# Graph attention scores: 32-row products with keys block-diagonal over two heads, and masks stored by tile

## The chip, the cores and the metric

The kernel runs on one core of a Trainium2 chip (trn2). The metric is the time on the device in microseconds of one execution; the median over several runs counts. TensorE (PE) multiplies matrices into PSUM and loads its weights separately (PEld in the profile). VectorE (DVE), ScalarE (ACT) and GpSimd (POOL) do elementwise work, and SyncE (SP) issues most of the DMAs. All data are fp32.

## What is computed

Two layers follow one another on x, 64 batches of 64 tokens with 256 features: a graph attention in two directions, then a transformer block with modulation. The change concerns the graph attention. Cut to that:

```python
def _gat_attention(self_feat, cond_adj, label_bias, Wq, bq, Wk, bk, Wout, bout):
    B, N, F = self_feat.shape          # 64, 64, 256
    ng = min(NONGT, N)                 # 20 keys per batch
    dh = F // H                        # 16 heads of 16
    kv = self_feat[:, :ng]
    qh = (self_feat @ Wq.T + bq).reshape(B, N, H, dh)
    kh = (kv @ Wk.T + bk).reshape(B, ng, H, dh)
    aff = jnp.einsum('bnhd,bmhd->bnhm', qh, kh) * (1.0 / np.sqrt(dh))
    mask = cond_adj[:, :, None, :] > 0
    aff = jnp.where(mask, aff, NEG) + label_bias[:, :, None, :]
    w = jax.nn.softmax(aff, axis=-1)
    out_t = jnp.einsum('bnhm,bmf->bnhf', w, kv)
    ...
for d in range(2):
    A = adj_f if d == 0 else jnp.swapaxes(adj_f, 1, 2)
    A = A[:, :, :NONGT, :]             # 11 labels per pair
    cond = A.sum(-1)
    vb = A @ w_bias + b_bias
    output = output + _gat_attention(self_feat, cond, vb, ...)
```

The second layer is layer norm with a modulation, 16-head attention over the 64 tokens of a batch, and an MLP with a hidden width of 1024, each with a gated residual.

## The kernel before

**Tiling.** Tokens are worked on in groups: one of 4 batches, seven of 8 and one of 4. A group is cut into tiles of 128 tokens, two batches each (`s` counts them), 32 tiles in all. Feature-major tensors have 256 features in two chunks `c` of 128 partitions. The schedule is written out by hand: the order of the calls is the order of each engine's instructions.

**The pipeline.** `period(g)` runs the transformer attention of group g beside the graph attention of group g+1, the MLP of group g-1 and preparation of group g+2. Its unit is `slot`: block scores of one tile (`block_scores`, line 620), graph scores of one tile (`graph_scores`, line 458), and then, interleaved, the softmax of both on DVE, ACT and POOL, the transposes and weighted sums of the tiles of the slot before, and pieces of the MLP as filling (`fills`). `boundary` stands between groups. `start` works on the graph tiles of the first group, and on the first two of the second group, ahead of the first slots; there are 28 slots with both kinds of scores, and `finish` has no graph scores.

**Graph scores.** For each direction `d` and chunk `c`, `graph_q` (lines 422 and 423) makes the queries qT, and `graph_k` (lines 407 and 411) the keys kT, feature-major; 128 partitions hold eight heads of 16. Heads are separated by a block-diagonal form of the keys. `graph_keys` multiplies kT with a mask that keeps one of four heads in each of four copies, so that 64 partitions (four heads) against 4 x 20 = 80 columns give the scores of four heads in one product. It is one POOL instruction a tile (line 441), except in the second group, where it is four ACT instructions (line 436). `graph_scores` then makes 16 products a tile: 2 directions, 2 chunks, 2 row groups `r` of 64 partitions, 2 batches `s`. The queries are the weights (64 rows, 64 columns), the key blocks the moving operand (80 columns).

**PSUM.** Two pairs of banks, sca and scb, take the scores. Block scores use columns 0 to 255 of all four banks: the row groups 0 and 1 of 32 partitions have the two banks of sca, 2 and 3 those of scb. Graph scores lie behind them in the same banks; direction 0 is in sca and direction 1 in scb, and each row group has its own bank of the pair.

**Softmax of the graph tile.** `mask_step` sums the labels of the adjacency on DVE (line 347, count) and the weighted labels (line 352), and makes from them `keep` (line 356) and `term` (lines 359 and 360), stored by direction, then tile, then key. `graph_masked` multiplies PSUM by keep, one DVE instruction a direction (line 469), and adds term on POOL (line 474). `graph_exp` takes maxima and subtracts on DVE (lines 479, 480), and exponentiates on ACT (line 481). `graph_normal` sums, inverts and scales (lines 486 to 488). `graph_turned` transposes on PE (line 496); `graph_output` multiplies with the values (line 514), adds on DVE (line 523), ACT (line 524) and POOL (line 525).

**Other lines of the prediction.** Block scores' maxima and subtraction on DVE are lines 631 and 633, their scaling on POOL line 645 (pr), the transposes line 656 (ppT), the weighted sum line 667 (pao). Line 605 makes the block-diagonal keys of the transformer attention on POOL, 32 partitions and two heads a product. Line 242 is the projection of the conditioning. Lines 737 and 747 are the two products of the MLP.

The order of the heads in the columns of Wq and Wk is arranged on the host, in `kernel`, so that the products leave the heads in natural order.

Of the kernel before, what the change touches and what calls it, by code (L numbers as in the profile page):

```python
# [9 lines left out]
F32 = mybir.dt.float32  # L10
I32 = mybir.dt.int32
AF = mybir.ActivationFunctionType
ALU = mybir.AluOpType
AX = mybir.AxisListType
# [3 lines left out]
P = 128  # L18
B, N, D = 64, 64, 256
H, HD = 16, 16  # L20
M = 20
L = 11
# [24 lines left out]
def graph_attention_then_dit_block(  # L47
# [22 lines left out]
    nc = tc.nc  # L70
# [5 lines left out]
    two = ctx.enter_context(tc.tile_pool(name="two", bufs=2))  # L76
# [118 lines left out]
    hmask4 = const.tile([P, 4], F32, name="hmask4")  # L195
    nc.gpsimd.tensor_tensor(hmask4, hmask[:, 0:4], hmask[:, 4:8], ALU.add)

    hmask2 = const.tile([P, 2], F32, name="hmask2")
# [139 lines left out]
    def mask_step(g, i):  # L338
        G = groups[g]
        rows = G.nt * M  # L340
        d, what = divmod(i, 3)
        if i == 0:
            G.cnt = small.tile([P, 2 * NT * M], F32, tag="cnt", name="cnt", bufs=1)[:, 0 : 2 * rows]
            G.vb = small.tile([P, 2 * NT * M], F32, tag="vb", name="vb", bufs=1)[:, 0 : 2 * rows]
        a3 = G.adj[d].rearrange("p j (m l) -> p (j m) l", l=L) if d < 2 else None
        if d < 2 and what == 0:
            nc.vector.tensor_reduce(G.cnt[:, ts(d, rows)], a3, AX.X, ALU.add)
        elif d < 2 and what == 1:

            nc.vector.tensor_tensor(a3.bitcast(F32), a3, wb.unsqueeze(1).to_broadcast([P, rows, L]), ALU.mult)  # L350
        elif d < 2:
            nc.vector.tensor_reduce(G.vb[:, ts(d, rows)], a3.bitcast(F32), AX.X, ALU.add)
        else:
            keep_f = small.tile([P, 2 * NT * M], F32, tag="keep", name="keep")[:, 0 : 2 * rows]
            G.keep = keep_f.rearrange("p (d j m) -> p d j m", d=2, m=M)
            nc.vector.tensor_scalar(keep_f, G.cnt, 0.0, None, ALU.is_gt)
            term_f = small.tile([P, 2 * NT * M], F32, tag="term", name="term")[:, 0 : 2 * rows]
            G.term = term_f.rearrange("p (d j m) -> p d j m", d=2, m=M)
            nc.vector.tensor_scalar(term_f, keep_f, -1.0, -NEG, ALU.add, ALU.mult)
            nc.vector.scalar_tensor_tensor(term_f, G.vb, bb, term_f, ALU.add, ALU.add)  # L360

# [67 lines left out]
    def graph_keys(g, j):  # L429

        G = groups[g]
        G.kblk = getattr(G, "kblk", {})
        kblk = G.kblk[j] = two.tile([P, 2, 2, 2, 4 * M], F32, tag="kblk", name="kblk")
        if g == 1:
            for h in range(4):
                nc.scalar.activation(
                    kblk.rearrange("p d c s (h m) -> p h (d c s) m", h=4)[:, h],
                    G.kT[:, j].rearrange("p d c (s m) -> p (d c s) m", s=2), AF.Copy, scale=hmask4[:, h : h + 1],
                )
            return  # L440
        nc.gpsimd.tensor_tensor(
            kblk.rearrange("p d c s (h m) -> p (d c s) h m", h=4),
            G.kT[:, j].rearrange("p d c (s m) -> p (d c s) m", s=2).unsqueeze(2).to_broadcast([P, 8, 4, M]),
            hmask4.unsqueeze(1).unsqueeze(3).to_broadcast([P, 8, 4, M]), ALU.mult,
        )

    def graph_scores(g, j, sc, first=4 * N):

        G = groups[g]
        t = Tile()  # L450
        t.g, t.j = g, j
        t.pa = [p_[:, :, ds(first, 8 * M)] for p_ in sc]
        kblk = G.kblk[j]
        for d in range(2):
            for c in range(2):
                for r in range(2):
                    for s in range(2):
                        nc.tensor.matmul(  # L458
                            t.pa[d][ts(s, N), r, ts(c, 4 * M)],
                            G.qT[ts(r, 64), d, c, ds(j * P + s * N, N)],  # L460
                            kblk[ts(r, 64), d, c, s, :], start=True, stop=True,
                        )
        return t

    def graph_masked(t):
        G, j = groups[t.g], t.j
        t.w = two.tile([P, H, 2, M], F32, tag="w", name="w")
        for d in range(2):
            nc.vector.tensor_tensor(  # L469
                t.w[:, :, d, :].rearrange("p (r h) m -> p r h m", r=2),  # L470
                t.pa[d].rearrange("p r (h m) -> p r h m", h=8),
                G.keep[:, d, j, :].unsqueeze(1).unsqueeze(1).to_broadcast([P, 2, 8, M]), ALU.mult,
            )
        nc.gpsimd.tensor_tensor(t.w, t.w, G.term[:, :, j, :].unsqueeze(1).to_broadcast([P, H, 2, M]), ALU.add)  # L474

    def graph_exp(t):
        wf = t.w.rearrange("p h d m -> p (h d) m")
# [287 lines left out]
    def slot(e, c, e_next, c_next, before, fill, late=False):  # L765
        Eb, Cb = before
        fill("p")
        sc = [pair("pa", "sca"), pair("pb", "scb")] if e or c else None
        E = block_scores(*e, sc) if e else None
        C = graph_scores(*c, sc) if c else None  # L770
        fill("p2")
        if Eb:
# [6 lines left out]
        if c_next and c_next[0] != 1:  # L779
            graph_keys(*c_next)  # L780
        if E:
            block_exp(E)
        if c_next and c_next[0] == 1:
            graph_keys(*c_next)
        if C:
            graph_masked(C)
# [31 lines left out]
    def boundary(g, before):  # L818
# [8 lines left out]
        if c_on:  # L827
            graph_v(g + 1, 1)
            if g == 1:
                half_normed(1, 3)  # L830
            for i in {1: (3, 1, 2, 4), 2: (1, 2, 4)}.get(g, (4, 5, 6)):
                mask_step(g + 1, i)
# [14 lines left out]
        if g <= 2:  # L847
            mask_step(g + 1, 5)
            mask_step(g + 1, 6)
# [48 lines left out]
        if c_on:  # L898
            graph_keys(g + 1, 0)
# [137 lines left out]
    def start():  # L1037
# [19 lines left out]
        for d in range(2):  # L1057
            for c in range(2):
                graph_q(0, d, c)
        sc = [pair("pa", "sca"), pair("pb", "scb")]  # L1060
        t0 = [graph_scores(0, 0, sc), graph_scores(0, 1, sc, 0)]
        for t in t0:
            graph_masked(t)
# [45 lines left out]
        graph_q(1, 1, 1)  # L1109
        sc = [pair("pa", "sca"), pair("pb", "scb")]  # L1110
        t1 = [graph_scores(1, 0, sc), graph_scores(1, 1, sc, 0)]
        for t in t1:
            graph_masked(t)
# [208 lines left out]
```

## Time and profile before

| | us |
|---|---|
| median of 3 runs | 672.87 |
| lowest, highest | 672.36, 674.28 |
| span of the profiled execution | 672.5 |

The span goes from the first to the last instruction of one profiled execution; durations are taken from it. The groups that the change touches, with their number of instructions and the mean time of one:

| line, engine | what | count | ns of one |
|---|---|---|---|
| 458 PE | graph scores, matmuls of 64x64, 80 columns | 1024 | 230 to 241 |
| 458 PEld | their weight loads | 1024 | 133 |
| 620 PE | block scores, 32x64, 128 columns | 1024 | 281 |
| 441 POOL | key blocks, 640 elements | 28 | 1252 |
| 436 ACT | key blocks of the second group, 160 elements | 16 | 416 |
| 469 DVE | scores times keep, 320 elements | 64 | 482 |
| 474 POOL | plus term, 640 elements | 32 | 1547 |
| 347 DVE | counts, up to 880 elements in | 18 | up to 1060 |
| 352 DVE | label bias, up to 880 elements in | 18 | up to 1071 |

How to read the views: a matmul's duration contains its way through the array, so durations of neighbouring matmuls overlap and can't be summed; their starts show the rate. An fp32 product appears as two pairs of load and matmul. A row of the timeline merges instructions of a line that follow closely: its start, its length, the engine, line and operation, output and inputs, shapes, and x how many; brackets give the idle time of the engine before it and what ended it. A row of the table by stretches gives, behind the length, the busy time and number of instructions of PE, PEld, DVE, ACT and POOL, then the granted clock of PE, the share of DMA and GB/s.

### The profile page before, as it was taken

The numbers are of one execution on the slowest core, as the hardware profiler recorded it, in microseconds if no ns is written. First come the engines' busy times: TensorE is split into PE (matmuls) and PEld (weight loads), VectorE is DVE, ScalarE is ACT, GpSimd is POOL, SyncE is SP. The second block draws the span as 40 slices with busy tenths as digits, with TensorE's granted clock in tenths as the row PEclk, the third lists the DMA queues.
The fourth block names the chain that finished last, engine by engine and source line by source line (L and its number), as shares of the span: only waits on it lengthen the run. The fifth ranks groups of instructions, "written<-read, shape, count | busy, mean of one in ns | idle before, by whom it ended". The sixth has DMA issues, their size and how long they took to land.

```text
span 672.5 us, 15456 instructions
## 1 busy us (share of the span) xinstructions
PE 657.7 (98%) x6422; PEld 405.7 (60%) x6422; DVE 473.3 (70%) x863; ACT 354.5 (53%) x627; POOL 369.9 (55%) x366
## 2 busy tenths in 40 slices
PE   8999898999999999999999999999999999999997
PEld 7657656775555555556556555555565575566446
DVE  4988866997777677775876867876778766666221
ACT  3355437663665437644476436664376544864412
POOL 5555447666674466654584556754766555545210
PEclk9999899999999999999999999999999999999999
DMA  7636031004000220004000041002100000000000
GB/s 244 201 90 203 22 104 18 18 22 135 17 2 34 90 68 17 18 17 156 1 18 17 22 153 17 1 18 73 42 9 12 19 25 2 2 2 17 17 16 32
DMA packets 34655, 33.42 MB, mean 50 GB/s; under 512 B 5625, under 2 KB 28409, under 8 KB 34585
## 3 DMA queue, kind: packets, MB, share of 16 engines
q1 hardware_dynamic: 34104, 32.33, 15.5%
q8 instruction: 51, 0.84, 0.6%
q14 instruction: 20, 0.16, 0.1%
q10 hardware_dynamic: 416, 0.09, 0.1%
q0 software_dynamic: 64, 0.01, 0.0%
HBM read 25.59 MB, written 6.83 MB: 48 GB/s over the span
## 4 chain that ended last, share of the span: by engine, by line
PE 86%; DVE 7%; ACT 3%; POOL 2%; issue 1%; DMA 1%; SPq 0%; DVEq 0%; ACTq 0%; POOLq 0%
PE py L747 15%; PE pu L737 15%; PE pqT L422 8%; PE pqk L582 8%; PE ppT L656 4%; PE pv L590 4%; PE pwT L496 3%; PE pf L324 3%; PE pproj L692 3%; PE po L514 3%; PE pk L407 2%; PE pao L667 2%; PE pv L371 2%; PE sca L620 2%; PE phT L560 2%; PE pxT L533 2%
## 5 line engine op out<-in xcount | busy, mean ns | idle before, releaser
L747 PE MATMUL py<-u,w 128*128 128x512 f32 (+1 forms) x272 | 118.3, 562 | 0.2 <-ACT u L739 0.2
L737 PE MATMUL pu<-h2T,w 128*128 128x512 f32 (+1 forms) x256 | 108.9, 570 | 0.4 <-ACT v L597 0.4
L645 POOL TENSOR_TENSOR pr<-pr,sm 128x1024 f32<-128x1024 f32 x32 | 60.9, 1902 | 73.0 <-DVE sm L644 53.5
L474 POOL TENSOR_TENSOR w<-w,term 128x640 f32<-128x640 f32 x32 | 49.4, 1547 | 71.1 <-DVE w L469 39.5
L737 PEld LDWEIGHTS pu<-h2T,w 128*128 128x128 f32 x256 | 47.6, 190 | 48.2 <-issue 42.6
L747 PEld LDWEIGHTS py<-u,w 128*128 128x128 f32 x272 | 47.7, 190 | 36.9 <-issue 33.2
L422 PE MATMUL pqT<-sfT,wq 128*128 128x512 f32 (+1 forms) x144 | 61.7, 558 | 0.3 <-DVE y L715 0.3
L739 ACT ACTIVATE u<-pu,vec 128x512 f32<-128x512 f32 (+1 forms) x72 | 43.1, 640 | 33.5 <-PE pu L737 33.3
L582 PE MATMUL pqk<-hT,wqkv 128*128 128x512 f32 (+1 forms) x144 | 59.5, 550 | 0.5 <-POOL hT L569 0.4
L631 DVE TENSOR_REDUCE mx<-sca 128x8 f32<-128x512 f32 x32 | 22.0, 688 | 48.8 <-PE sca L458 47.4
L481 ACT ACTIVATE w<-w 128x640 f32<-128x640 f32 x32 | 23.6, 736 | 56.9 <-DVE w L480 55.9
L641 DVE TENSOR_REDUCE sm<-pr 128x16 f32<-128x1024 f32 x32 | 38.9, 1216 | 20.3 <-ACT pr L637 20.0
L423 ACT ACTIVATE qT<-pqT,vec 128x512 f32<-128x512 f32 (+1 forms) x36 | 23.0, 639 | 51.8 <-PE pqT L422 51.7
L659 ACT COPY pT<-ppT 128x512 f32<-128x512 f32 x64 | 34.5, 591 | 26.4 <-PE ppT L656 26.4
L637 ACT ACTIVATE pr<-pr 128x1024 f32<-128x1024 f32 x32 | 33.8, 1057 | 27.2 <-DVE pr L633 27.0
L546 POOL TENSOR_TENSOR rstd<-rstd,mhalf 128x2 f32<-128x2 f32 x32 | 23.3, 727 | 41.7 <-DVE rstd L545 40.8
L583 ACT ACTIVATE qk<-pqk,vec 128x512 f32<-128x512 f32 (+1 forms) x36 | 23.0, 639 | 43.0 <-PE pqk L582 43.0
L488 POOL TENSOR_TENSOR w<-w,sm 128x640 f32<-128x640 f32 x32 | 44.1, 1380 | 1.9 <-DVE sm L487 1.8
L551 DVE TENSOR_SCALAR xn<-xn,mv,rstd 128x256 f32<-128x256 f32 x64 | 37.9, 632 | 10.0 <-POOL rstd L546 10.0
L542 DVE BATCH_NORM_STATS2 st<-xn 128x6 f32<-128x256 f32 x64 | 26.1, 408 | 24.3 <-ACT xn L535 24.2
L525 POOL TENSOR_TENSOR xT<-xT,sfT 128x256 f32<-128x256 f32 x32 | 23.2, 726 | 34.1 <-ACT sfT L524 29.0
L500 ACT COPY wT<-pwT 80x512 f32<-80x512 f32 x64 | 33.9, 581 | 13.0 <-PE pwT L496 12.9
(148 smaller groups left out, 1432.5 us busy)
## 6 DMA issues: line engine op xcount, KB each, us to landing
xT<-in_x_t SPq DMA_DIRECT2D x7, 512.0 KB
out<-xT SPq DMA_DIRECT2D x14, 256.0 KB
a_d<-in_adj SPq DMA_DIRECT2D x7, 440.0 KB
a_d<-in_adj_t SPq DMA_DIRECT2D x7, 440.0 KB
x_g<-in_x SPq DMA_DIRECT2D x5, 512.0 KB
vblk<-vd SPq DMA_DIRECT2D x28, 80.0 KB
w<-in_w SPq DMA_DIRECT2D x2, 1024.0 KB
vd<-v_sb SPq DMA_DIRECT2D x7, 256.0 KB
```

Source lines behind the costliest of these rows:

```text
L422: nc.tensor.matmul(pq, wq_sb[d][:, k, ts(c, P)], G.sfT[:, k, :], start=(k == 0), stop=(k == 1))
L474: nc.gpsimd.tensor_tensor(t.w, t.w, G.term[:, :, j, :].unsqueeze(1).to_broadcast([P, H, 2, M]), ALU.add)
L488: nc.gpsimd.tensor_tensor(wf, wf, sm.unsqueeze(2).to_broadcast([P, 2 * H, M]), ALU.mult)
L500: nc.scalar.copy(t.wT[:, ts(q4, 4), :], pt[0 : 4 * M, :].rearrange("p (i t) -> p i t", i=4))
L551: nc.vector.tensor_scalar(key.xn[:, i, :], key.xn[:, i, :], key.mv[:, i, 0:1], key.rstd[:, i : i + 1], ALU.subtract, ALU.mult,)
L582: nc.tensor.matmul(pp, wqkv_sb[:, k, ds(i * D + c * P, P)], G.hT[:, k, 0 : G.T], start=(k == 0), stop=(k == 1))
L641: nc.vector.tensor_reduce(t.sm, t.pr, AX.X, ALU.add)
L645: nc.gpsimd.tensor_tensor(t.pr, t.pr, t.sm.unsqueeze(2).to_broadcast([P, H, N]), ALU.mult)
L659: nc.scalar.copy(t.pT[:, ts(q4, 4), :], pt.rearrange("p (i t) -> p i t", i=4))
L737: nc.tensor.matmul(pu, w1_sb[:, k, ts(m, P)], G.h2T[:, k, 0 : G.T], start=(k == 0), stop=(k == 1))
L739: nc.scalar.activation(G.u[m], pu, AF.Gelu, bias=col("b1", m))
L747: nc.tensor.matmul(G.py, w2_sb[:, m, ts(c, P)], G.u[m], start=(m == 0), stop=(m == 7))
```

## The change

Graph scores become 32 products of 32 rows a tile. The key blocks hold two heads in place of four: 40 columns instead of 80, and half the size. The row groups `q` of 32 partitions take the four banks of sca and scb (q 0 and 1 in sca, 2 and 3 in scb), and both directions of a row group lie in its bank, with the direction inside the head: chunk, head, direction, key. An output is therefore two runs of 20 columns, 40 apart. The weights are 32 rows of queries and 64 columns. The position in the array is given: row 32q, column 64s, the same as for the block scores.

`keep` and `term` are stored by tile, then direction, then key, so that the 40 values of a tile lie together; the reductions that make the count and the label bias write runs of 20 accordingly. The masked product is cut by row groups instead of directions: each of the two DVE instructions still has 320 elements, and writes a contiguous half of `w`. The sum on POOL takes the 40 values as one run. Key blocks are made with the mask for two heads: one POOL instruction of 320 elements, or two ACT instructions in place of four. On the host the heads of Wq and Wk take the order that the transformer attention has already.

```diff
@@ mask_step
+        a4 = G.adj[d].rearrange("p j (m l) -> p j m l", l=L) if d < 2 else None
+
+        def by_direction(flat):
+            return flat.rearrange("p (j d m) -> p j d m", d=2, m=M)[:, :, d]
+
         if d < 2 and what == 0:
-            nc.vector.tensor_reduce(G.cnt[:, ts(d, rows)], a3, AX.X, ALU.add)
+            nc.vector.tensor_reduce(by_direction(G.cnt), a4, AX.X, ALU.add)
...
-            nc.vector.tensor_reduce(G.vb[:, ts(d, rows)], a3.bitcast(F32), AX.X, ALU.add)
+            nc.vector.tensor_reduce(by_direction(G.vb), a4.bitcast(F32), AX.X, ALU.add)
...
-            G.keep = keep_f.rearrange("p (d j m) -> p d j m", d=2, m=M)
+            G.keep = keep_f.rearrange("p (j r) -> p j r", j=G.nt)
...
-            G.term = term_f.rearrange("p (d j m) -> p d j m", d=2, m=M)
+            G.term = term_f.rearrange("p (j r) -> p j r", j=G.nt)
@@ graph_keys
-        kblk = G.kblk[j] = two.tile([P, 2, 2, 2, 4 * M], F32, tag="kblk", name="kblk")
+        kblk = G.kblk[j] = two.tile([P, 2, 2, 2, 2 * M], F32, tag="kblk", name="kblk")
         if g == 1:
-            for h in range(4):
+            for h in range(2):
                 nc.scalar.activation(
-                    kblk.rearrange("p d c s (h m) -> p h (d c s) m", h=4)[:, h],
-                    G.kT[:, j].rearrange("p d c (s m) -> p (d c s) m", s=2), AF.Copy, scale=hmask4[:, h : h + 1],
+                    kblk.rearrange("p d c s (h m) -> p h (d c s) m", h=2)[:, h],
+                    G.kT[:, j].rearrange("p d c (s m) -> p (d c s) m", s=2), AF.Copy, scale=hmask2[:, h : h + 1],
                 )
             return
         nc.gpsimd.tensor_tensor(
-            kblk.rearrange("p d c s (h m) -> p (d c s) h m", h=4),
-            G.kT[:, j].rearrange("p d c (s m) -> p (d c s) m", s=2).unsqueeze(2).to_broadcast([P, 8, 4, M]),
-            hmask4.unsqueeze(1).unsqueeze(3).to_broadcast([P, 8, 4, M]), ALU.mult,
+            kblk.rearrange("p d c s (h m) -> p (d c s) h m", h=2),
+            G.kT[:, j].rearrange("p d c (s m) -> p (d c s) m", s=2).unsqueeze(2).to_broadcast([P, 8, 2, M]),
+            hmask2.unsqueeze(1).unsqueeze(3).to_broadcast([P, 8, 2, M]), ALU.mult,
         )
@@ graph_scores
         for d in range(2):
             for c in range(2):
-                for r in range(2):
+                for q in range(4):
+                    out4 = t.pa[q // 2][:, q % 2].rearrange("p (c h d m) -> p c h d m", c=2, h=2, d=2)
                     for s in range(2):
                         nc.tensor.matmul(
-                            t.pa[d][ts(s, N), r, ts(c, 4 * M)],
-                            G.qT[ts(r, 64), d, c, ds(j * P + s * N, N)],
-                            kblk[ts(r, 64), d, c, s, :], start=True, stop=True,
+                            out4[ts(s, N), c, :, d], G.qT[ts(q, 32), d, c, ds(j * P + s * N, N)],
+                            kblk[ts(q, 32), d, c, s, :].rearrange("p (h m) -> p h m", h=2),
+                            start=True, stop=True, tile_position=(32 * q, 64 * s),
                         )
@@ graph_masked
-        for d in range(2):
+        wf = t.w.rearrange("p h d m -> p h (d m)")
+        for i in range(2):
             nc.vector.tensor_tensor(
-                t.w[:, :, d, :].rearrange("p (r h) m -> p r h m", r=2),
-                t.pa[d].rearrange("p r (h m) -> p r h m", h=8),
-                G.keep[:, d, j, :].unsqueeze(1).unsqueeze(1).to_broadcast([P, 2, 8, M]), ALU.mult,
+                wf[:, ts(i, 8)].rearrange("p (q h) m -> p q h m", q=2),
+                t.pa[i].rearrange("p q (h m) -> p q h m", h=4),
+                G.keep[:, j].unsqueeze(1).unsqueeze(1).to_broadcast([P, 2, 4, 2 * M]), ALU.mult,
             )
-        nc.gpsimd.tensor_tensor(t.w, t.w, G.term[:, :, j, :].unsqueeze(1).to_broadcast([P, H, 2, M]), ALU.add)
+        nc.gpsimd.tensor_tensor(wf, wf, G.term[:, j].unsqueeze(1).to_broadcast([P, H, 2 * M]), ALU.add)
@@ kernel
-    order = np.arange(D).reshape(2, 2, 4, HD).transpose(1, 0, 2, 3).reshape(-1)
-
     order1 = np.arange(D).reshape(4, 2, 2, HD).transpose(1, 0, 2, 3).reshape(-1)
...
     for name in ("Wq", "bq", "Wk", "bk"):
-        l0[name] = l0[name][:, order]
+        l0[name] = l0[name][:, order1]
```

## The prediction

> **What bounds the kernel now.** I read the busy table and the slices of the page first, then the busy times of four stretches, then the timeline of one slot.
>
> ```profile
> PE 657.7 (98%) x6422; PEld 405.7 (60%) x6422; DVE 473.3 (70%) x863; ACT 354.5 (53%) x627; POOL 369.9 (55%) x366
> ...
> PEclk9999899999999999999999999999999999999999
> ```
>
> ```profile
> 0.00:120.00 120.00, 110.87 (x1168) 78.47 (x1169) 91.82 (x166) 57.06 (x115) 67.50 (x77) 0.99 0.40 124
> 120.00:505.00 385.00, 384.90 (x3859) 227.48 (x3857) 288.15 (x516) 216.27 (x370) 229.56 (x219) 1.00 0.14 42
> ```
>
> PE is the bound: between 120 and 505 us it is busy 384.90 of 385.00 us at the full granted clock, while DVE, ACT and POOL are at 75%, 56% and 60%. There, PE time saved is kernel time saved. In the first 120 us PE is idle for 9 us, so savings can be lost there. The change touches PE at line 458, in 28 slots where the graph scores directly follow the block scores, and twice in the start for two tiles at a time. One of the slots in the timeline (start and length in us; PEld rows are weight loads):
>
> ```profile
> 208.41 0.15 PEld L620 LDWEIGHTS sca<-kb,qk 32*64 32x64 f32 x4 [0.76 <-POOL w L488]
> ...
> 208.49 0.15 PEld L620 LDWEIGHTS scb<-kb,qk 32*64 32x64 f32 x4
> ...
> 208.68 0.29 PE L620 MATMUL sca<-kb,qk 32*64 32x128 f32 x4
> ...
> 208.79 0.29 PE L620 MATMUL sca<-kb,qk 32*64 32x128 f32 x4
> 208.81 0.29 PE L620 MATMUL scb<-kb,qk 32*64 32x128 f32 x4
> 209.03 0.35 PEld L458 LDWEIGHTS sca<-kblk,qT 64*64 64x64 f32 x16 [0.17 <-issue]
> 209.03 0.51 PE L458 MATMUL sca<-kblk,qT 64*64 64x80 f32 x16
> ...
> 209.36 0.46 PE L458 MATMUL scb<-kblk,qT 64*64 64x80 f32 x16
> 209.61 0.69 DVE L631 TENSOR_REDUCE mx<-sca 128x8 f32<-128x512 f32 x1 [3.15 <-PE sca L458]
> 209.74 0.86 PEld L656 LDWEIGHTS ppT<-ident,pr 128*128 128x128 f32 x8
> ```
>
> Each fp32 product shows as two load+matmul pairs, so 16 products are 32 pairs. The block scores (32-row products) run in rounds of eight: rounds start 0.11 us apart (208.68, 208.79), and inside a round four matmuls lie within 0.29 - 0.268 = 0.02 us (one takes 268 ns), so a start every 7 ns. The graph scores (64-row) run in rounds of four: the scb group is 0.46 long, one matmul 0.229, so four rounds span 0.23, or 0.069 a round. Columns explain both: 109/128 and 69/80 ns are 0.85 ns a column. The last block matmul starts at 208.83 and streams until 208.94, yet the first graph load starts at 209.03: 0.09 us of nothing. The last graph matmul starts at 209.59 (209.36 + 0.46 - 0.229), streams 0.07, and again 0.09 passes until 209.74. From the last block matmul to the next load: 0.91 us, the same within 1 ns in 27 of the 28 slots (the other waits for POOL behind it).
>
> **The change on PE.** 32 products of 32 rows and 40 columns replace 16 of 64 rows and 80: 64 pairs, in eight rounds of eight, on the array tiles and the four banks that the block scores use. What limits a round:
> - streaming: 40 x 0.85 = 34 ns;
> - starting eight pairs: 8 x 6.7 = 54 ns, from the 7 ns above;
> - the weights: each array tile needs a new load of 64 columns per round. In the block scores the loads of the second round start 0.055 after those of the first (208.41; 208.46). For loads longer than their matmul in steady state, the nearest row is the time projection, 128-column weights under 64-column matmuls:
>
> ```profile
> 50.13 0.97 PEld L242 LDWEIGHTS pt<-siluT,wt_sb 128*128 128x128 f32 x8
> ```
>
> (0.97 - 0.19)/7 = 0.111 us a load; half the columns make 55 ns, and a few ns more if part of it is fixed for each load. I take 58, the upper end, since this row is the steady one. So a round costs 58 ns where it cost 69, and there are still eight.
>
> The larger part is the seam. Both score stages now have one array layout (32x64). Inside the block scores no seam of 0.09 stands between rounds, nor between the attended product and the graph output (lines 667 to 514, both 32 columns wide): there loads at 228.46 start while the earlier matmuls run. So I take the 0.09 before the graph scores as gone, and their first loads as hidden under the last block round. The new slot: first graph matmul at 208.79 + 0.109 = 208.90; last at 208.90 + 7 x 0.058 + 7 x 0.0067 = 209.35; plus 0.034 streaming and 0.09 of seam, next load at 209.47 instead of 209.74. **0.27 us saved a slot** (0.29 with rounds of 55 ns).
>
> In the start, both pairs of graph tiles wait in mid-stage for the last qT activation (line 423), before and after; behind that wait lie ten rounds: 10 x 0.011 + 0.034 = 0.15 us each. The first pair's gain ends in the 1.0 us wait before the transposes at 25.98, so I count one.
>
> Where is the slot's gain lost? Where the next PE wait hangs on a chain that starts in the same slot. At 112.94 the transposes wait 2.03 us for POOL's pr, whose chain begins with the block scores: nothing gained from slot 110. The slots at 49.4 (PE waits 0.89 at 54.80 for a masked product) and 572.5 (0.48 idle before 578.0) I count out likewise. Elsewhere the slack is large: pr of the slot before 208 ended at 203.62 + 1.90 = 205.5, needed at 209.74.
>
> Sum: 25 x 0.27 + 0.15 = **6.9 us**; at most 28 x 0.29 + 0.3 = 8.4. The profiled span is 672.5 us, 0.4 under the median of the runs; 672.87 - 6.9 = **666.0 us**.
>
> **A rule against it.** TensorE: Matmul & The Clock Gate, section "Back-to-back issue gap", gives 1 to 64 columns a floor of about 60 cycles, some 25 ns start to start, and TensorEngine Tiling (Array Packing), section "Performance Considerations", warns against taking the tiling factor from a dimension that is already small: exactly what 80 to 40 columns does. By that floor as an estimate, 64 pairs would take 1.6 us a slot against 0.56 now, some 29 us in all. The trace has matmuls of different array tiles 7 ns apart, so it doesn't hold across tiles here.
>
> **The parts beside PE**, all off the path while PE is the bound:
> - Key blocks (line 441): POOL's 28 instructions of 1.25 us go from 640 to 320 columns. The 256-column product of line 605 takes 0.61; so 0.61 to 1.25, and I take 0.7: 15 us less on POOL, ahead of the block keys that the scores wait for. On ACT (line 436) eight fewer instructions of 0.42 us. Worth 0 to 0.5 us of PE waits; I take 0.
> - Masked product (line 469): same 320 elements, output now contiguous; 0.42 (line 523, 256 contiguous elements) to 0.48. POOL's sum (line 474): 1.27 (line 488, contiguous) to 1.55. Zero; if DVE became the bound, the most is 64 x 0.06 = 4 us.
> - Count and bias reductions (lines 347, 352): 36 instructions of up to 1.06 us now write in runs of 20. Line 469 already writes such runs, at 1.5 ns an element, no dearer than line 523's 1.6; so 0, at worst 36 x 0.1 = 4 us of DVE time, under DVE's 25% of idleness.
> - Waits: mx (line 631) waits for the last matmul into sca, which used to be the middle of the stage (209.31) and now lies four starts before its end (209.32): unchanged. Behind it on DVE stand the subtractions and masked products. PE's next use of the result is the 4 us slack above. An interleaved store into PSUM (two runs of 20) has no row: 0, or twice the streaming, 68 ns a round, which makes the slot's gain 0.16 and the sum 4.2.
>
> **Rivals.**
> 1. *The seam stays* (the first graph load waits until the array is empty, whatever the layout). Then 209.03 + 0.055 + 7 x 0.058 + 0.047 + 0.124 = 209.66: 0.08 a slot, 2.2 us, **670.7**. For it: every change of line with another layout shows it. Against: 667 to 514.
> 2. *The gain is taken by waits*: PE arrives 0.27 earlier and waits for DVE or POOL. Under 2 us kept, **671 to 673**. Against: nearly no PE idleness from 120 to 505, slack of microseconds.
> 3. *Slower: the pairs can't be fed.* No row shows more than about 64 pairs in a run, and the densest long one (line 667: 32 pairs from 228.04 to 228.46) gives 13.4 ns a pair, though there streaming explains it. At 13.6 ns a pair a round is 0.109, the slot ends 0.134 later: 28 x 0.134 + 2 x 10 x 0.04 = 4.6, **677.5**. It decides from 11.5 ns a pair: the 0.91 us less 0.06 before the first and 0.12 behind the last leave 0.72 for 63 steps. Against: after PE had stood 0.46 us for ACT's qk, eight pairs of line 620 start from 48.98 to 49.06: 10 ns a pair from a standstill.
>
> **Chances.** Forecast 0.70 (664.4 to 668.7, the interleaved store included), seam 0.10, waits 0.08, feed 0.12. The range, 663.8 to 671.0, takes in the first two. A measurement of this kernel tells about 0.3%, 2 us, from no change. Faster: 0.70 + 0.07 of the seam + 0.01 = 0.78; same: 0.03 + 0.07 = 0.10; slower 0.12.
>
> **What would show it.** Line 458 with 2048 matmuls of 32x40; its first load in a slot no longer behind a gap of 0.09 after line 620; rounds 55 to 58 ns apart; last block matmul to next load 0.64 us instead of 0.91; line 441 near 0.7. The forecast is wrong if a round takes over 92 ns, if the gap before line 458 stays, or if new PE idleness between 120 and 505 us exceeds 2 us.

## The result and the profile after

The changed kernel takes **684.75 us** (median of 4 runs, 683.91 to 685.44) where the kernel before takes 673.57 beside it: ratio 1.0164, interval 1.0145 to 1.0184. It is slower by 1.6%, outside the range and on the other side of the forecast. Two experiments further down, e2 and e13, have a profile only of a disturbed execution in which matmuls took two to two and a half times as long; their times and ratios come from their other runs.

From the page of the changed kernel, the busy table and the chain that ended last:

```profile
span 683.5 us, 17497 instructions
...
PE 662.4 (97%) x7446; PEld 413.9 (61%) x7446; DVE 471.0 (69%) x863; ACT 352.2 (52%) x619; POOL 354.6 (52%) x366
...
PE 82%; DVE 7%; ACT 4%; another core or an unknown queue 2%; POOL 2%; issue 1%; DMA 1%; SPq 0%; DVEq 0%; ACTq 0%; POOLq 0%
```

The same two stretches as before (length, then busy time and number of instructions of PE, PEld, DVE, ACT, POOL, granted clock, DMA share, GB/s), and what PE waited for in the second one:

```profile
0.00:120.00 120.00, 111.43 (x1422) 80.50 (x1422) 90.17 (x165) 55.01 (x107) 64.68 (x77) 0.99 0.40 124
120.00:505.00 385.00, 378.18 (x4320) 225.79 (x4311) 280.63 (x505) 207.06 (x358) 210.69 (x212) 1.00 0.14 42
```

```profile
PE pv L597 <- issue: 4.9, 3, 2.7
PE pu L744 <- ACT v L604: 1.1, 1, 1.1
PE ppT L663 <- ACT u L746: 0.6, 2, 0.3
```

PE is idle for 6.82 us between 120 and 505 us where it was idle for 0.10. The granted clock is 1.00 over that stretch in both, but not all through it (below). The chain shows a new entry of 2%, work that the profile has no engine for. Starts of the same activation (line 739 before, 746 after) date the loss: 207.1 against 208.1 us (+1.0), 286.2 against 292.1 (+5.9), 444.3 against 455.3 (+10.9), and 11 at the end. So some 5 us each are lost in two places, around 255 and around 418 us, and the 25 slots that should have gained 6.7 us gain nothing.

**The score stage.** One slot of the changed kernel, as in the prediction (PE and PEld rows of the timeline):

```profile
209.80 0.24 PEld L464 LDWEIGHTS sca<-kblk,qT 32*64 32x64 f32 x5
...
209.83 0.29 PE L627 MATMUL scb<-kb,qk 32*64 32x128 f32 x4
209.91 0.25 PE L464 MATMUL sca<-kblk,qT 32*64 32x40 f32 x4
...
210.55 0.28 PE L464 MATMUL scb<-kblk,qT 32*64 32x40 f32 x4
...
210.76 0.20 PEld L663 LDWEIGHTS ppT<-ident,pr 128*128 128x128 f32 x2
```

The seam ahead of the graph scores is gone: their first load starts while the last block matmuls are starting, and their first matmul follows 0.06 us after the last block matmul (209.85). But from there to the last graph matmul (210.60) it is 0.69 us for 64 pairs, and the next load comes at 210.76, as late as before. In numbers from the trace, median slot:

| ns | before | after |
|---|---|---|
| last block matmul to first graph matmul | 197 | 63 |
| first to last graph matmul | 555 | 692 |
| last graph matmul to the next load | 158 | 153 |
| last block matmul to the next load | 910 | 907 |

The seam gives 134 ns and the longer run of products takes 137. From the first load of the block scores to the last graph matmul, called the score stage below, it is 1179 ns before and 1181 after.

**The two holes.** The timeline around 250 us:

```profile
249.03 0.37 SPq L293 DMA_DIRECT2D nzd<-nz  x1
...
251.06 0.27 PE L464 MATMUL scb<-kblk,qT 32*64 32x40 f32 x4
251.26 3.10 PEld L597 LDWEIGHTS pv<-wqkv,hT 128*128 128x128 f32 x15
251.26 3.29 PE L597 MATMUL pv<-wqkv,hT 128*128 128x256 f32 x14
257.27 0.59 PE L597 MATMUL pv<-wqkv,hT 128*128 128x256 f32 x2 [2.72 <-issue]
...
257.30 0.34 SPq L294 DMA_DIRECT2D nzb<-nzd  x1
257.36 0.69 DVE L638 TENSOR_REDUCE mx<-sca 128x8 f32<-128x512 f32 x1 [8.35 <-remote]
```

PE stops in the middle of the value product (line 597), with 14 of 16 matmuls issued, though the trace shows nothing that it waits for. DVE's maximum waits for scores that PE finished at 251.3, and starts 6 us later. Both go on at 257.3, when SP issues the load of nzb, which waits for one thing: the write of the flags of nonzero rows (line 293), 512 words of 4 bytes from SBUF to DRAM, begun at 249.03. In the kernel before the same write takes as long and nothing waits beside it: mx starts 0.06 us after the last product into sca has ended (250.07).

```profile
247.80 0.37 SPq L293 DMA_DIRECT2D nzd<-nz  x1
...
250.13 0.69 DVE L631 TENSOR_REDUCE mx<-sca 128x8 f32<-128x512 f32 x1 [2.36 <-PE sca L458]
...
256.65 0.34 SPq L294 DMA_DIRECT2D nzb<-nzd  x1
```

The second hole is of the same kind, beside the write that begins at 412.09: PE stops twice on line 597 and goes on 0.4 us before the load is issued. Right behind it the granted clock is 0.50 for 3.4 us, which by an estimate from that share costs 1.7 of the 5 us lost there (row by stretches, as above):

```profile
417.76 0.59 PE L597 MATMUL pv<-wqkv,hT 128*128 128x256 f32 x2 [0.59 <-issue]
...
419.91 1.09 PE L597 MATMUL pv<-wqkv,hT 128*128 128x256 f32 x2 [1.55 <-issue]
...
420.30 0.34 SPq L294 DMA_DIRECT2D nzb<-nzd  x1
```

```profile
419.90:423.30 3.40, 3.39 (x5) 1.57 (x5) 2.80 (x5) 0.28 (x1) 0.00 (x0) 0.50 0.02 7
```

The other writes that score products fall into, at 169.99, 333.03 and 495.62, pass without a stop.

### The profile page after: what moved, and what is told of

Its sections match the earlier page's. It is cut to its first block, busy times and chain, and to the rows that moved or that the text cites. A ratio compares the mean times of both kernels' runs of the same rounds, so it can differ in the third digit from the quotient of the medians.

```text
span 683.5 us, 17497 instructions
## 1 busy us (share of the span) xinstructions
PE 662.4 (97%) x7446; PEld 413.9 (61%) x7446; DVE 471.0 (69%) x863; ACT 352.2 (52%) x619; POOL 354.6 (52%) x366
## 4 chain that ended last, share of the span: by engine, by line
PE 82%; DVE 7%; ACT 4%; another core or an unknown queue 2%; POOL 2%; issue 1%; DMA 1%; SPq 0%; DVEq 0%; ACTq 0%; POOLq 0%
PE py L754 15%; PE pu L744 13%; PE pqT L427 8%; PE pqk L589 8%; PE ppT L663 5%; PE pwT L503 4%; PE pf L324 3%; PE pproj L699 3%; PE pv L597 3%; PE po L521 3%; PE pao L674 2%; PE pk L412 2%; PE pv L376 2%; PE pxT L540 2%; PE phT L567 2%
## 5 line engine op out<-in xcount | busy, mean ns | idle before, releaser
L744 PE MATMUL pu<-h2T,w 128*128 128x512 f32 (+1 forms) x256 | 110.6, 576 | 1.7 <-ACT v L604 1.7
L558 DVE TENSOR_SCALAR xn<-xn,mv,rstd 128x256 f32<-128x256 f32 x64 | 34.1, 573 | 10.0 <-POOL rstd L553 10.0
L663 PE MATMUL ppT<-ident,pr 128*128 128x128 f32 x256 | 36.1, 284 | 4.0 <-POOL pr L652 3.2
```

The source lines that it names most:

```text
L558: nc.vector.tensor_scalar(key.xn[:, i, :], key.xn[:, i, :], key.mv[:, i, 0:1], key.rstd[:, i : i + 1], ALU.subtract, ALU.mult,)
L663: nc.tensor.transpose(pt[:, ts(i, P)], t.pr[:, ts(q4 * 4 + i, 2), :].rearrange("p h m -> p (h m)"), ident)
L744: nc.tensor.matmul(pu, w1_sb[:, k, ts(m, P)], G.h2T[:, k, 0 : G.T], start=(k == 0), stop=(k == 1))
```

## The experiments

Two questions followed: what holds PE up (theory W: the flags' write), and why the stage gained nothing (issue theory: a small product costs a fixed time to issue, whatever stands beside it). Rival causes were the masks' new order, the place at which PE's instructions are fetched, the store's two runs, and tile rounds limited by their weights.

### e1: the flags written once

```diff
-        nzd = dram.tile([GT], F32, tag="nzd", name="nzd")[0 : G.T]
-        nc.sync.dma_start(nzd.rearrange("(j p) -> p j", p=P), nz)
-        nc.sync.dma_start(G.nzb, nzd.partition_broadcast(P))
+        if g == 3:
+            groups[3].nzd = dram.tile([GT], F32, tag="nzd", name="nzd")
+            nc.sync.dma_start(groups[3].nzd.rearrange("(j p) -> p j", p=P), nz)
+        nc.sync.dma_start(G.nzb, groups[3].nzd[0 : G.T].partition_broadcast(P))
```

> The changed kernel, but the flags of nonzero rows are written to DRAM (512 elements of 4 bytes) only for the fourth group; later groups read that copy, so the write of their own flags is left out. In the changed kernel PE stands still at 254.2 and 416.8 us until that write has landed, and about 4.2 us are lost at each of the two places, with 0.7 behind each. Theory W (PE's stream is held up by this write): both stalls are gone, 673 to 675 us in place of 684.8. Rival S (the stalls come from the scores themselves, whatever is in flight): 683 to 686.

Measured: 674.92 us, ratio to the kernel before 1.0011 (0.9992 to 1.0031). PE has no wait left between 120 and 505 us. Taking five of the six writes away takes the whole loss away: W holds. It also shows what the change does without them: nothing.

### e2, e3: all PE instructions moved by 128

```diff
         conditioning_of_self()
+        for _ in range(32):
+            nc.tensor.matmul(warm[0:1, 0:1], ones[:, 0:1], ones[:, 0:1], start=True, stop=True)
         self_product(0, 0)
```

The changed kernel:

> The changed kernel with 32 more one-column products in the start, where PE waits for a weight: 128 more PE instructions ahead of all that follows, half of what one fetch of PE instructions brings (16 KB, 256 instructions). Nothing else moves. Theory A (what decides is where the fetches of PE's instructions fall, against the 8 us in which the flags' write is under way): the stalls at the fourth and sixth period's beginning go elsewhere or vanish; 673 to 681. Rival D (what decides is how many PE instructions are started in those 8 us): the same two stalls, 684 to 686.

The kernel before:

> The kernel before with the same 32 one-column products in the start. Theory A (position of the fetches): a stall of some 4 us can turn up at a period's beginning, 673 to 683, and the fetches that fall into the flags' write change. Rival D (number of PE instructions): no stall, 673 to 674.5.

Measured: e2 685.5 us, ratio 1.0158 (1.012 to 1.0196); e3 675.43 us, 1.0006 (0.9987 to 1.0025). The changed kernel stays slow and the kernel before stays as it is, so the loss is no accident of one alignment. Where e2's hold-ups lie can't be read. In e3's trace a fetch of PE's instructions begins inside each of the five writes that score products fall into, three of them 3.2 to 3.7 us long, and PE stops in none.

### e4: only the masks by tile

The diff's parts in `mask_step`, with `keep` and `term` read in their new order by the old `graph_masked`; the scores as before.

> The kernel before with one part of the change: keep and term stored by tile, the reductions writing runs of 20; scores and key blocks as before. Theory: costs nothing, lines 347 and 352 stay at about 1.06 us, 672.5 to 674.5. Rival: strided writes on DVE cost 0.1 us each and push the softmax chains, 675 to 678.

Measured: 673.98 us, ratio 1.0011 (0.999 to 1.0032). The masks cost nothing, as predicted.

### e5: the flags in runs of 16 bytes

```diff
-        nc.sync.dma_start(nzd.rearrange("(j p) -> p j", p=P), nz)
+        nc.sync.dma_start(nzd.rearrange("(p j) -> p j", p=P), nz)
@@ self_cond
-        nc.gpsimd.tensor_tensor(tq, G.nzb.rearrange("p (b n) -> p b n", n=N), q, ALU.mult)
+        nc.gpsimd.tensor_tensor(
+            tq.rearrange("p (j s) n -> p j s n", s=2), G.nzb.rearrange("p (s n j) -> p j s n", s=2, n=N),
+            q.rearrange("p (j s) n -> p j s n", s=2), ALU.mult,
+        )
```

> The changed kernel, with the flags of nonzero rows written to DRAM as 128 runs of 16 bytes (each partition its four flags in a row) in place of 512 single words of 4 bytes; POOL reads them back in that order (line 315). Nothing is left out. Theory W (PE's two stalls of about 5 us in all at 254 and 417 us come from the flags' write, whose landing takes 8 us because it is 512 single words): the write lands in about a quarter of the time, the stalls at 254 and 417 go, 674 to 676 us. Rival R (the landing takes 8 us whatever the run length, as a fixed latency of a write to DRAM beside other traffic): the write still takes 8 us, the stalls stay, 684 to 686 us.

Measured: 674.76 us, ratio 1.0023 (1.0013 to 1.0032). SP's rows in its timeline, and the stretch from 120 to 505 us:

```profile
249.53 0.34 SPq L293 DMA_DIRECT2D nzd<-nz  x1
251.20 0.34 SPq L294 DMA_DIRECT2D nzb<-nzd  x1
```

```profile
120.00:505.00 385.00, 384.81 (x4467) 231.80 (x4463) 286.79 (x516) 215.37 (x370) 220.09 (x220) 1.00 0.14 42
```

The load that waits for the write is issued 1.67 us after it in place of 8.26, and PE is busy again for 384.81 of 385.00 us. So it is the landing of single words, not a write as such, and the loss is mended without leaving work out. It isn't their number either: the last group has half the tokens, and its write of 256 words lands as late as one of 512 (7.95 us in the changed kernel); as 128 runs of 8 bytes it takes 3.63 us here, where those of 16 bytes take 1.4 to 2.0. The Trainium skill ("DMA: Bandwidth & Descriptors", section "Specifications") says that transfers under 512 bytes are done as read-modify-write; both forms here are under that, and 8.26 against 1.67 us is a factor of five between them.

### e10: the same repair in the kernel before

> The kernel before, with the flags written in 128 runs of 16 bytes, nothing else. Control for the repaired changed kernel. If the write held nothing up before the change, as its trace reads, the time is that of the kernel before within 0.2%, and what the repaired changed kernel loses or gains against it is the scores alone; if the write cost something before as well, it is up to 3 us faster.

Measured: 674.54 us, ratio 1.0017 (0.9997 to 1.0037). The repair gives the kernel before nothing, so its write held nothing up. Repaired against repaired, each in its own series, the two kernels stand at 1.0023 and 1.0017 of the kernel before: the new scores are worth nothing that can be measured.

### e6: the write 8 us earlier

`nonzero_rows(g + 2)` moves from the end of the boundary to behind the token norms:

```diff
             for j2, k in enumerate(K):
                 norm_tokens(k, A.xT, j2)
                 norm_stats(k)
+            if a_on and g > 1:
+                nonzero_rows(g + 2)
...
-        if a_on and g > 1:
-            nonzero_rows(g + 2)
```

> The changed kernel, with the flags' row sums, write and load (lines 288 to 294) issued in the middle of the boundary between two periods, behind the token norms, in place of at its end, some 8 us earlier. Nothing is left out. Theory D (the write does harm only while PE issues the dense small products of lines 464 and 627 at the head of a period's first slot; products of 128 rows and 512 columns in the boundary pass): the write has landed before that slot, both stalls go, 674 to 676 us. Rival A (any write of the flags holds PE up wherever PE stands at a fetch of instructions): stalls of the same 4 us move into the boundary, 680 to 686 us.

Measured: 690.21 us, ratio 1.0238 (1.0216 to 1.026), slower than both theories had it. In the profile the write goes out 7.4 us ahead of the scores (249.7 and 257.1 us) and its load follows 1.0 us behind their start. PE's waits between 160 and 420 us:

```profile
PE phT L567 <- DVE xn L558: 7.0, 8, 1.5
PE scb L464 <- issue: 1.7, 1, 1.7
```

One hold-up is left, at 176 us, where the write (166.2 to 177.4) still covers the scores. Four-microsecond stops in the boundary, as rival A had them, don't appear; that part speaks for D. 7.0 us of the time go to something that neither had: row sums (1.21 us) and comparison (0.38 us) now stand on DVE ahead of the normalisation that PE's transposes (line 567) wait for.

### e7: the graph products twice

```diff
-        for d in range(2):
+        for d in (0, 1, 0, 1):
```

> The changed kernel with every graph score product issued twice (64 products of 32 rows a slot in place of 32, the second pass overwriting the first with the same values). Issue theory (a product of 32 rows takes 22.5 ns whatever stands beside it, 11.3 ns a pair of load and matmul): the score stage, last block product to the end of the graph products, grows by 32 x 22.5 = 720 ns a slot. Weights theory (a round of 8 pairs on disjoint tiles is limited by one tile's load and stream of 58 ns, as the prediction had it, and the rest is a fixed cost of entering the stage): it grows by 8 x 58 = 464 ns a slot.

Measured in a single run 743.53 us. In slots without a hold-up the score stage takes 1821 ns where the changed kernel takes 1181: 32 products more cost 640 ns, **20.0 ns a product**, or 10.0 ns a pair; rounds of 58 ns would have cost 464. The price of the issue theory holds, a little below its 22.5, which had counted some 80 ns of getting started. Its cause isn't shown by this: a limit on something that all array tiles share, the loads of the weights for one, could cost the same. One tile's load and stream alone is an unlikely limit, since the kernel before loads the same 64 columns in rounds of 69 ns, where eight pairs here take 80. PE's waits between 120 and 505 us name the largest part of the remaining time:

```profile
PE scb L464 <- issue: 10.9, 4, 3.5
PE sca L464 <- issue: 7.7, 2, 5.8
```

These are stops inside the graph products themselves. Five of the six fall into the flight of a write of flags, and a seventh, of 4.2 us, into the last one at 546 us: with more products PE is held up in four of the five writes that the score products fall into, not in two. The sixth, 1.9 us at 217 us, has no write beside it; the only transfer in flight is the fetch of PE's own instructions, begun at 216.6. The granted clock is part of the rest: 0.96 between 120 and 505 us.

### e8: the columns of a product side by side

```diff
-                    out4 = t.pa[q // 2][:, q % 2].rearrange("p (c h d m) -> p c h d m", c=2, h=2, d=2)
+                    out4 = t.pa[q // 2][:, q % 2].rearrange("p (d c n) -> p d c n", d=2, c=2)
...
-                            out4[ts(s, N), c, :, d], G.qT[ts(q, 32), d, c, ds(j * P + s * N, N)],
-                            kblk[ts(q, 32), d, c, s, :].rearrange("p (h m) -> p h m", h=2),
+                            out4[ts(s, N), d, c], G.qT[ts(q, 32), d, c, ds(j * P + s * N, N)],
+                            kblk[ts(q, 32), d, c, s, :],
```

> The changed kernel with each product's 40 columns stored side by side in PSUM in place of as two runs of 20 (the masked product of line 477 then runs as four instructions of DVE in place of two). Nothing is left out. Issue theory: the store's pattern has no part in it, 720 ns from the first graph load to the last matmul in a slot, as in the changed kernel. Rival (the two runs of the store slow each product): under 600 ns.

Measured: 798 ns from the first graph load to the last matmul in a slot, 799 in the changed kernel. (The 720 of the expectation counts from the second load, which starts 0.08 us after the first.) The store's two runs cost nothing. The kernel's time of 688.46 us in one run holds hold-ups that end at 257, 344 and 505 us and longer chains on DVE, and says nothing on this question.

### e9: the kernel before with more products in one slot of a period

```diff
-        for d in range(2):
+        for d in (0, 1, 0, 1) if g > 1 and j == 0 else (0, 1):
```

> The kernel before, with the 16 graph score products of the first slot of a period (groups 2 to 7) issued twice, the second time with the same values. PE then issues as many loads and matmuls at the head of that slot as the changed kernel does (192), while the flags' write of 512 single words is on its way. The products themselves cost 6 x 0.55 = 3.3 us. Theory N (the number of PE instructions issued while the write is on its way decides whether PE stands still): stalls of PE of 1 to 6 us appear in the trace before the write lands, 680 to 690 us. Rival L (something else of the change, its four banks or its 32-row tiles, is needed): no such stall, 676 to 678 us.

Measured: 696.11 us, ratio 1.0329 (1.0281 to 1.0377). The doubled stage is 553 ns longer, as computed, so 3.3 us are the products. The rest shows in its timeline at 255 us and in its waits between 120 and 505 us:

```profile
254.85 0.37 SPq L293 DMA_DIRECT2D nzd<-nz  x1
...
260.91 0.70 PE L590 MATMUL pv<-wqkv,hT 128*128 128x256 f32 x2 [0.41 <-issue]
263.30 0.19 PEld L590 LDWEIGHTS pv<-wqkv,hT 128*128 128x128 f32 x1 [2.09 <-issue]
...
263.80 0.34 SPq L294 DMA_DIRECT2D nzb<-nzd  x1
```

```profile
PE pv L590 <- issue: 8.2, 5, 2.4
PE pu L737 <- ACT v L597: 2.9, 2, 1.9
```

It is the same hold-up, on the same line, beside the same write, in a kernel with none of the change's banks, tiles or masks; it comes in three of the five writes (at 175, 261 and 346 us), and PE goes on 0.5 to 1.8 us before the waiting load is issued. What this run and the change have in common is the number of PE instructions at the head of the slot, behind the start of the write: 192 loads and matmuls of scores in place of 128.

### e12: the changed kernel moved by 64 PE instructions

The diff of e2 with 16 in place of 32.

> The changed kernel with 16 products of one column (64 PE instructions) added at the start, so that all later PE instructions stand 64 further in the blocks of 256 in which they are fetched. If the place of a fetch in the stream decides which windows of the flags' write hold PE up, the stalls (before: windows at 249 and 412 us) come in other windows or go; if not, they stay in these two. The time is 676 to 688 us.

Measured: 685.96 us in one run. The hold-ups have gone from the writes at 249 and 412 us to those at 327 and 492 us. So which writes hold PE up goes with where PE stands in its stream of instructions, and the sum comes out alike in this run.

### e14: the write after the products

```diff
-        nz = small.tile([P, NT], F32, tag="nz", name="nz", bufs=1)[:, 0 : G.nt]
-        nc.vector.tensor_scalar(nz, rs, 0.0, None, ALU.not_equal)
+        G.rs = rs
+        if g == 3:
+            flags_sent(g)
+
+    def flags_sent(g):
+        G = groups[g]
+        nz = small.tile([P, NT], F32, tag="nz", name="nz", bufs=1)[:, 0 : G.nt]
+        nc.vector.tensor_scalar(nz, G.rs, 0.0, None, ALU.not_equal)
@@ period
-                    "f1": [...] + (conds if g == 1 else []),
+                    "f1": [...] + (conds if g == 1 else ahead(flags_sent)),
...
-                    "d2": masks(1) + conds if g > 1 else [],
+                    "d2": masks(1) if g > 1 else [],
...
-                    "f1": ahead(self_product, 0),
+                    "f1": (conds if g > 1 else []) + ahead(self_product, 0),
```

> The changed kernel, its flags written as 512 single words as in it, but only after the score products of the next period's first slot: the comparison of line 291 moves behind the masked product in that slot, the write and load follow it, and the flags' two readers (line 315) move from that slot's end to the next slot. Nothing is left out. Theory N (PE instructions issued while the write is on its way decide): PE then issues under 190 instructions in the 8 to 10 us, as in the kernel before, no stall, 674 to 677 us. Rival (the write holds PE up wherever it falls): stalls of 2 to 4 us remain, 680 to 690 us.

Measured: 678.84 us, ratio 1.007 (1.0046 to 1.0093): 6 us faster than the changed kernel, 2 us over the expectation. PE's waits between 120 and 505 us:

```profile
PE pf L330 <- DVE sfT L337: 1.8, 3, 1.0
PE sca L470 <- issue: 0.5, 1, 0.5
PE scb L470 <- issue: 0.5, 1, 0.5
```

The long hold-ups are gone with the write as slow as ever (8.2 to 10.7 us to the load); 1.0 us remains where it still overlaps the next slot's scores, and 1.8 us is new, from the flags' readers being late. The count of PE instructions during the flight was not under 190 as expected but some 190 to 250, so the bare count doesn't decide. That the dense products must come early in the flight is a guess that fits this run, not shown: in e6 PE stops for 1.7 us at 174.8 although the write had begun 8.6 us before. In both runs such a stop late in the flight stays short, and the write lands soon after.

### e11, e13: block and graph products in turn

Both have the repair of e5, and issue one block product and two graph products by turns:

```diff
+    def scored(E, C):
+        todo = (E.todo if E else []) + (C.todo if C else [])
+        if E and C:
+            todo = []
+            for i in range(16):
+                c8 = i // 8 * 8
+                todo += [E.todo[i], C.todo[c8 + (i + 3) % 8], C.todo[16 + c8 + (i + 6) % 8]]
+        for out, lhsT, rhs, at in todo:
+            nc.tensor.matmul(out, lhsT, rhs, start=True, stop=True, tile_position=at)
```

> The changed kernel with the flags in runs of 16 bytes and, in a slot with both, the 16 block and 32 graph products of a slot issued in turn (one block product on tile i, two graph products on tiles i+3 and i+6) in place of one after the other. Issue theory (20 ns a product is the limit of a stage of small products, and the block products alone are limited by their own streams, 16 in 0.43 us): 48 products take 0.96 us and 0.08 us to get going, 1.04 us in place of 1.23 us, 25 slots x 0.15 to 0.19 = 4 to 5 us less than the repaired kernel, 670 to 671 us. Rival (tiles collide, or the products of 128 columns hold the queue up): no gain, 674 to 676 us.

Measured: 679.88 us, ratio 1.0095 (1.0062 to 1.0128). The stage takes 1310 ns in place of 1181: slower, so the rival holds. e13 puts the graph products on tiles i+4 and i+2:

> The same mix of block and graph products as in the run before, with the two graph products of a step on tiles i+4 and i+2 in place of i+3 and i+6: on each tile the next product after a block product then comes four steps later in place of two. Issue theory with collisions taken away: a block product keeps its tile for up to 0.21 us (two passes of 0.107 us), two steps of 60 ns were too short for it, four are not; 48 x 20 + 80 = 1.04 us from the first load to the last matmul in place of 1.31 us (mixed) and 1.18 us (one after the other), some 4 us under the repaired kernel, 670 to 672 us. Rival (a mixed stage is slow for a reason that is not the distance on a tile): 1.25 to 1.35 us, 678 to 681 us.

Measured: 681.52 to 683.63 us, ratio 1.013 (1.0111 to 1.015), no better than e11. By the time, distance on a tile was not the reason. The issue theory fails in both, by 0.27 us a stage in e11 and by 10 us or more in e13's time, so a fixed time a product, whatever stands beside it, is not what limits a mixed stage. Why products of 128 and 40 columns by turns are slower than one kind after the other stays open; no version tried here beats the kernel before.

## Why the prediction was wrong

**The step that failed** is the price of a round: "So a round costs 58 ns where it cost 69". It took the load of the weights as the limit, by a row of 128-row products (0.111 us a load, halved), and the start of a pair as 6.7 ns, from four matmuls in a row. Both are too low for a long run: further pairs take 10.0 ns each (e7), so eight take 80 ns, more than the 69 of a round before, and the first 64 take 11.0 ns a step. In the terms of the forecast's sum, from the last block matmul on: the first graph matmul 0.07 us later (measured 0.06), the run of 64 pairs 0.45 (measured 0.69), the end with its seam 0.12 (measured 0.15). So the slot gains 0.003 us and not 0.27. The 7 ns was the distance inside a burst of matmuls whose loads had gone ahead.

**The second step** is a term that the sum doesn't have: what a transfer already in flight does to PE when the stage beside it gets denser. It left the flags' write out, and with it some 10 us (684.75 in the changed kernel, 674.92 in e1). The prediction's own sign, new PE idleness of over 2 us between 120 and 505 us, shows it: 6.7 us.

No row of the kernel before settled the price. The longest dense run (line 667) had 13.4 ns a pair and was limited by streaming. Rival 3's "10 ns a pair from a standstill" agrees with e7 by luck: its 0.08 us run from the first load, at 48.98, to the eighth matmul, and the eight matmuls themselves start within 0.05 us, 7 ns apart, a burst again.

**The rivals.** Rival 1, the seam that stays, is refuted. Rival 3 named the step: the pairs can't be fed faster. Its break-even of 11.5 ns a pair becomes 11.0 with the measured entry and end, and the run takes 11.0, so the slot changes by 3 ns. Its price of 13.6 ns and its 677.5 us were too dear; that the kernel came out slower, as it says, comes from the write and is no merit of it. The rule that the prediction set aside (the Trainium skill, "TensorE: Matmul & The Clock Gate", section "Back-to-back issue gap", about 25 ns start to start for small products) was applied to load-and-matmul pairs. For a whole fp32 product it would give, as an estimate from that page, 32 x 25 = 800 ns for 32 products. The runs show 640 for 32 more products (e7).

**What was right.** The seam of 0.09 us goes, since the first graph load now overlaps the last block matmuls. POOL's key blocks take 0.72 us (0.7 predicted) and give PE nothing. The masks cost nothing (e4), and the interleaved store costs nothing (e8). DVE's maximum was predicted unchanged in the slot and starts 0.18 us later (1.38 us after the stage's first load, 1.20 before); nothing on PE waits for that.

**What no case held.** The 11 us come from a transfer that the change doesn't touch: with denser products beside it, the flags' write holds PE up. Of the loss, 4.9 and 5.0 us are the two hold-ups with what follows them (PE waiting for ACT's v, then the transposes, and in the second the 3.4 us at half the clock), shown by e1 and e5, which take them away, and by e9, which makes them in the kernel before. The remaining 1.0 us comes between 112 and 134 us, where the granted clock is 0.50 for 3.4 us from 112.7. The profiles of e4 and e10, without the new scores, have such a stretch there too (from 111.5 and 113.6) and lose 1.2 and 1.4 us; that of e12, with them, has none and loses nothing. So it isn't laid to the change.

**What stays open** is what PE lacks in a hold-up. One lead is the fetch of its instructions, 16 KB at a time. During the writes most such fetches take 3 to 4.3 us in place of about 1. The stops of the changed kernel, e9 and e12 begin at most some 100 PE instructions behind the start of one, and so does the stop at 217 us in e7, without a write. But the stops at 274.3 and 546.0 us in e7 and at 174.8 in e6 begin before the next fetch does (275.1, 548.1 and 177.9). The hold-up at 254 us outlasts its fetch (251.7 to 255.4). And fetches as slow pass without a stop in other writes, before (250.2 us, 4.3 long), after (172.9) and in e3. The other lead is late word from PE: at 251.3 DVE already misses the word of finished scores, 0.4 us before that fetch begins. But at 346 us in e9 PE stops though DVE's maximum had started on time (342.4). No run separated the two.

## What to carry to other kernels

The spacing inside a burst of four or eight products (7 ns a pair here) is not the price of a long run (10.0 to 11.0 ns). Where no row of the page shows a run of that length and shape, take the burst and the longest run as the two bounds (7 and 13.4 ns) and see whether the break-even (11.5 by the prediction) lies between them; if it does, the sign of the gain is open until a run like e7 measures the price. Here halving a product's size and doubling their number cost 137 ns a slot and gave back a seam of 134. Where a stage is made denser, list the DMAs in flight during it, above all writes of single words to DRAM: 128 runs of 16 bytes in place of 512 words cost a changed pattern on the reader and freed PE and DVE.

## What the hardware showed

A write of 512 words of 4 bytes to DRAM, 2 KB in all, takes 8.1 to 11.2 us until the load that waits for it is issued, though the trace has its data packets done within 1.3 us; one of 256 words takes 8.0 to 8.8 us. In 128 runs of 8 bytes it takes 3.5 to 4.0 us, in 128 runs of 16 bytes 1.4 to 2.1. During the slow landing another engine, which shares no data with it, can stand still: PE for up to 5.8 us (e7), and DVE, through late word from PE, for 5 to 8 us. Whether it does goes with how many score products PE issues at the head of the slot (of the five writes that they fall into, none in the kernel before, two in the changed kernel, three in e9, four in e7) and with where PE stands in its instructions (e12). Long runs of fp32 products of 32 rows, 64 columns of weights and 40 columns cost 20.0 ns a product (e7); what sets that price is not shown.
